# Five copies of the running counts in PSUM in an edge sort: one copy to SBUF for five chunks

## The chip, the cores and the metric

The kernel runs on one NeuronCore of one Trainium2 chip. The metric is the device time of one execution in microseconds; the kernel before has a median of 14442.03 us over 3 runs (14433.29 to 14450.2).

## The reference, cut to what matters

Four graph layers work on one graph of 12,500 nodes and 400,000 edges; each gathers node features by edge, makes a message, and adds the messages up by node.

```python
edge_index = jnp.stack([src, dst])
h = jnp.maximum(_layernorm(x, axis=-1), 0.0)
x = x + _L0_gnn_ref(h, edge_index, ...)          # x[s] * norm, segment_sum over d
...
x = x + _L1_gnn_ref(h, edge_attr_16, ..., src, dst, edge_type_90)
...
x = x + _L2_gnn_ref(h, edge_attr_4, edge_index, ...)
...
x = x + _L3_gnn_ref(h, src, dst, edge_weight)
```

Before the layers, the kernel sorts the edges by the pair of 128-node buckets that their destination and their source lie in: 98 x 98 pairs. This sort is what is changed. It is no part of the reference, and the order within a pair doesn't matter to it.

## The kernel before

A first pass (`hist`, to about 417 us) counts the edges of each pair of buckets; `cbase`, 98 x 98, holds the slot at which each pair begins. The sort itself walks over the edges in `NBE` = 125 blocks of 3200: `KE` = 25 chunks of 128 edges, one edge to a partition. `rec` in DRAM gets one record of 32 bytes per edge, at the slot of that edge. The slot is the running count of the edge's pair over all chunks before (`p_c`), plus the edge's rank among the equal keys of its own chunk.

For one block the steps are these, by the lines of the kernel before:

- ScalarE's queue issues the loads `keyb` (L508, 1.6 MB) and `db` (L511); SP's queue issues the loads of the edges' inputs (L503) and one piece of a clearing of DRAM buffers (L527, 1.5 MB).
- VectorE (DVE) makes `ohdt`, the one-hot of the destination bucket with buckets on partitions, in f32 (L516), the shifts and the packed word (L535 to L553), the product `pr` and its sum into `q` (L556, L557), and the one-hots `ohd` and `ohs` of destination and source bucket, in bf16 (L298, a helper that also makes `ohl`).
- 25 rounds, one for each chunk `k`: ScalarE copies the counts from PSUM, `c_sb <- p_c` (L573, 98 x 98 f32). PE adds the chunk's own counts to `p_c` (L574, `ohd` against `ohs`, bf16, accumulated in PSUM). PE looks up the counts for the chunk's edges, `p_l` (L576, `ohdt` against `c_sb`, f32). DVE makes the rank by comparing keys (`junk`, L579). The next copy has to wait until L574 has added, and L574 has to wait until the copy has read.
- After every five chunks DVE picks the count of each edge's source bucket: `own` (L583, 490 wide) and a reduction into `slot_f` (L584).
- After the 25 chunks DVE makes `ohl`, adds `slot_f` and `rank` (L589), and works out `slot` (L591 to L601). Then GpSimd (POOL) issues 25 indirect DMAs (L603), each of which scatters the 128 records of a chunk to `rec`.
- PE counts degrees of the block with 25 matmuls into `p_deg` (L475) from `ohd` and `ohl`, while the next block begins.

The tiles of the `sort` pool have two buffers each, those of `count` three, `p_l` three. `q` of a block shares its buffer with `q` of the block two earlier, and can be written when the scatters of that block have landed. A recording layer with a scheduler decides in which order the instructions of neighbouring blocks stand on each engine: for example DVE makes `ohdt` of the next block before it finishes `slot` of this one. On ScalarE the first copy of a block stands before that block's loads are issued, since it only needs the counts of the block before.

Of the kernel before, what the change touches and what calls it, by code (L numbers as in the profile page):

```python
# [30 lines left out]
F32 = mybir.dt.float32  # L31
# [4 lines left out]
ALU = mybir.AluOpType  # L36
AF = mybir.ActivationFunctionType
AX = mybir.AxisListType
# [6 lines left out]
P = 128  # L45
# [3 lines left out]
NB = 98  # L49
# [7 lines left out]
KE = 25  # L57
BE = P * KE
NBE = E // BE
UE = 5  # L60
KI = UE * KE

# [19 lines left out]
def gnn_kernel(  # L82
# [25 lines left out]
    nc = tc.nc  # L108
# [23 lines left out]
    ident = const.tile([P, P], F32, name="ident")  # L132
# [72 lines left out]
    def clear(acc, m, width):  # L205
        for c in range(0, width, 512):
            w = min(512, width - c)
            nc.tensor.matmul(acc[:m, c : c + w], zeros[:, :m], zeros[:, :w], start=True, stop=False,
                             skip_group_check=True)
# [59 lines left out]
    with ExitStack() as begin:  # L269
# [15 lines left out]
        cbase = base.tile([NB, NB], F32, name="cbase")  # L285
# [18 lines left out]
        with tc.tile_pool(name="hist", bufs=2) as hist, tc.tile_pool(name="hpsum", bufs=1, space=PSUM) as ps:  # L304
            p_cnt = ps.tile([NB, NB], F32, name="p_cnt")
            clear(p_cnt, NB, NB)
            for it in range(NBE // UE):
                e0 = it * UE * BE
                hi = {}
                for name, idx in (("d", dst), ("s", src)):  # L310
                    v = hist.tile([P, UE, KE], I32, name="v" + name)
                    nc.sync.dma_start(v, idx[e0 : e0 + UE * BE].rearrange("(u p k) -> p u k", u=UE, k=KE))
                    v = v.rearrange("p u k -> p (u k)")
# [9 lines left out]
                for v, row, dt in ((key, keyrow, F32), (hd, drow, BF16)):  # L323
# [4 lines left out]
                    nc.sync.dma_start(row[it * KI : (it + 1) * KI, :], tt)  # L328
                for u in range(UE):
                    sl = slice(u * KE, (u + 1) * KE)  # L330
                    ohd = hist.tile([P, KE, NB], BF16, name="ohd")
                    one_hot_n(ohd, hi["d"][:, sl, :], NB)
                    ohs = hist.tile([P, KE, NB], BF16, name="ohs")
                    one_hot_n(ohs, hi["s"][:, sl, :], NB)
                    for k in range(KE):
                        nc.tensor.matmul(p_cnt, ohd[:, k, :], ohs[:, k, :], start=False, stop=False,
                                         skip_group_check=True)
# [117 lines left out]
        with (  # L455
# [1 line left out]
            tc.tile_pool(name="count", bufs=3) as count,  # L457
            tc.tile_pool(name="spsum", bufs=1, space=PSUM) as ps,
        ):
            p_c = ps.tile([NB, NB], F32, name="p_c")  # L460
            nc.tensor.matmul(p_c, ident[:NB, :NB], cbase, start=True, stop=False, skip_group_check=True)
            p_deg = ps.tile([NB, P], F32, name="p_deg")
            clear(p_deg, NB, P)

# [8 lines left out]
            def count_degrees(oh):  # L473
                for k in range(KE if oh else 0):
                    mm = nc.tensor.matmul(p_deg, oh[0][:, k, :], oh[1][:, k, :], start=False, stop=False,  # L475
                                          skip_group_check=True)
                    if k == 0:
                        tc.keep_in_program_order(mm)
# [4 lines left out]
            for buf, src_z in ((buf1, zero_b), (buf2, zero_b), (buf3, zeros)):  # L483
                flat = buf.rearrange("(p g) c -> p (g c)", g=NG)
                m, step = flat.shape[1], src_z.shape[1]
                for c in range(0, m, 6 * step):
                    k, w = divmod(min(6 * step, m - c), step)
# [3 lines left out]
                    if w:  # L491
                        blank.append((flat[:, c + k * step : c + k * step + w], src_z[:, :w]))
            every = -(-len(blank) // (NBE - 1))

            degrees = None
            for blk in range(NBE):
                e0 = blk * BE
# [17 lines left out]
                ohdt = sort.tile([NB, BE], F32, name="ohdt")  # L515
# [47 lines left out]
                slot_f = sort.tile([P, KE], F32, name="slot_f")  # L563
                ohd = sort.tile([P, KE, NB], BF16, name="ohd")
                one_hot_n(ohd, hi["d"], NB, iota_p)
                ohs = sort.tile([P, KE, NB], BF16, name="ohs")
                one_hot_n(ohs, hi["s"], NB, iota_p)
                count_degrees(degrees)
                for kb in range(0, KE, 5):
                    p_l = ps.tile([P, 5, NB], F32, name="p_l", bufs=3)  # L570
                    for k in range(kb, kb + 5):
                        c_sb = count.tile([NB, NB], F32, name="c_sb")
                        nc.scalar.copy(c_sb, p_c)  # L573
                        nc.tensor.matmul(p_c, ohd[:, k, :], ohs[:, k, :], start=False, stop=False,  # L574
                                         skip_group_check=True)
                        nc.tensor.matmul(p_l[:, k - kb, :], ohdt[:, k * P : (k + 1) * P], c_sb,  # L576
                                         start=True, stop=True)
                        junk = count.tile([P, P], BF16, name="junk")
                        nc.vector.scalar_tensor_tensor(junk, keyb[:, k * P : (k + 1) * P], key[:, k : k + 1],  # L579
                                                       earlier_p, op0=ALU.is_equal, op1=ALU.mult,  # L580
                                                       accum_out=rank[:, k : k + 1])
                    own = count.tile([P, 5, NB], F32, name="own")
                    nc.vector.tensor_tensor(own, p_l, ohs[:, kb : kb + 5, :], op=ALU.mult)  # L583
                    nc.vector.tensor_reduce(slot_f[:, kb : kb + 5], own, axis=AX.X, op=ALU.add)  # L584
                ohl = sort.tile([P, KE, P], BF16, name="ohl")
                one_hot_n(ohl, lo_d, P, iota_p)
                degrees = (ohd, ohl)
# [24 lines left out]
        with (  # L612
# [51 lines left out]
            for g0 in range(0, NG, 35):  # L664
# [6 lines left out]
                for g in range(g0, g0 + nm):  # L671
                    nc.tensor.matmul(pm[:, g - g0, :], ht[:, (g - g0) * P : (g - g0 + 1) * P], mvx[:, g, :],
                                     start=True, stop=True)
# [625 lines left out]
```

## Time and profile before

| what | before |
| --- | --- |
| median of 3 runs | 14442.03 us |
| profiled execution, its own time | 14454.86 us |
| its span, first to last instruction | 14452.8 us |
| mean granted PE clock | 0.599 of full |
| PE, DVE, ACT, POOL busy | 50%, 64%, 17%, 49% |
| first and last start of L603 (the sort's scatters) | 479.1 us, 6969.2 us |
| L573 copies, one | 3125, 241 ns |
| L574 matmuls, one | 3125, 254 ns |
| L576 matmul passes (f32 takes two), one | 6250, 457 ns |
| L603 indirect DMAs on POOL, one | 3125, 966 ns |

The profile is of one execution. A group's row gives its busy time, the mean of one instruction in ns, and the idle time of its engine just before its instructions, with what ended most of that. "PEld" is PE's loading of weights, which overlaps its matmuls; ends of matmuls are modelled. "issue" and "remote" are waits for which the profile shows no instruction that ended them. In timeline rows the columns are the start in us, the duration in us, engine, line, operation and tiles, and in brackets the idle time before it with what ended it.

### The profile page before, as it was taken

How to read it: one execution, taken by the hardware profiler on the slowest of the kernel's cores; microseconds unless marked ns; L12 is line 12 of the kernel's file. 1: busy time of each engine (PE TensorE's matmuls, PEld its weight loads, DVE VectorE, ACT ScalarE, POOL GpSimd, SP SyncE). 2: the span in 40 equal slices, each digit the busy share in tenths (PEclk: the TensorE clock that was granted, in tenths of full speed). 3: DMA queues.
4: the chain of work that ended last, by engine and by line, in shares of the span. 5: the costliest groups of instructions: out<-in, count | busy, mean ns of one | idle time of the engine just before them, and what ended most of it. 6: DMA issues, size and time to landing. Idle time of an engine off the chain costs nothing. (4 is left out here: it accounts for less than half of the span.)

```text
span 14452.8 us, 284351 instructions
## 1 busy us (share of the span) xinstructions
PE 7195.8 (50%) x112895; PEld 6405.0 (44%) x112895; DVE 9312.5 (64%) x18267; ACT 2509.1 (17%) x7316; POOL 7108.7 (49%) x8252
## 2 busy tenths in 40 slices
PE   5433333333333333333223622688888566656677
PEld 5333333333333333333122422577776555546666
DVE  8544444444444444444445634999999989995799
ACT  0111111111111111111122222000000542201344
POOL 0344444444444444444386287377777425520476
PEclk7555555555555555555555555599999559955555
DMA  3222222222222222221576387433333326646543
GB/s 86 91 83 83 83 83 76 78 80 80 83 83 83 83 83 83 83 83 63 170 238 207 115 273 245 137 96 95 95 95 91 114 85 203 192 125 200 162 123 110
DMA packets 1100964, 1704.92 MB, mean 118 GB/s; under 512 B 660792, under 2 KB 727909, under 8 KB 1080779
## 3 DMA queue, kind: packets, MB, share of 16 engines
q1 hardware_dynamic: 746151, 737.61, 17.2%
q10 hardware_dynamic: 164704, 715.37, 14.6%
q0 software_dynamic: 188704, 233.01, 5.2%
q8 instruction: 906, 14.84, 0.4%
q14 instruction: 499, 4.09, 0.1%
HBM read 1079.99 MB, written 555.86 MB: 113 GB/s over the span
## 5 line engine op out<-in xcount | busy, mean ns | idle before, releaser
L603 POOL DMA_INDIRECT rec<-q,slot x3125 | 3019.6, 966 | 3532.6 <-issue 3469.1
L576 PEld LDWEIGHTS p_l<-c_sb,ohdt 98*128 98x128 f32 x6250 | 1606.3, 318 | 3288.2 <-issue 3039.2
L583 DVE TENSOR_TENSOR own<-p_l,ohs 128x490 f32<-128x490 f32 x625 | 418.1, 669 | 3390.4 <-PE p_l L576 2183.9
L574 PE MATMUL p_c<-ohs,ohd 128*98 128x98 bf16 x3125 | 794.2, 254 | 3518.0 <-issue 1512.5
L576 PE MATMUL p_l<-c_sb,ohdt 98*128 98x98 f32 x6250 | 1999.9, 457 | 242.5 <-DVE gran L591 200.0
L715 POOL DMA_INDIRECT buf<-msg,place x1188 | 1544.4, 1300 | 819.5 <-DVE msg L249 341.4
L573 ACT COPY c_sb<-p_c 98x98 f32<-98x98 f32 x3125 | 753.7, 241 | 5671.1 <-remote 2414.7
L769 DVE TENSOR_TENSOR oh<-lo,row 128x2304 bf16<-128x2304 bf16 x1070 | 1413.0, 1346 | 77.5 <-PEq L739 31.7
L1007 PE MATMUL pw<-wt,ot 128*128 128x256 bf16 x10692 | 1267.3, 273 | 374.5 <-DVE pr L1011 333.4
L1007 PEld LDWEIGHTS <-ot 128*128 128x128 fp8e4 x10692 | 1043.2, 98 | 575.6 <-issue 457.7
L1011 DVE TENSOR_TENSOR pr<-pw,hg 128x1536 f32<-128x1536 f32 x594 | 1041.3, 1753 | 145.6 <-POOL mm L1026 137.9
L747 PE MATMUL pg<-xg,o 128*128 128x16 bf16 (+1 forms) x33156 | 980.0, 173 | 288.6 <-DVE o L700 159.9
L747 PEld LDWEIGHTS <-o 128*128 128x128 fp8e4 x33156 | 938.6, 101 | 322.3 <-DVE o L700 169.5
L574 PEld LDWEIGHTS <-ohd 128*98 128x98 bf16 x3125 | 626.7, 201 | 693.7 <-DVE ohd L298 426.6
L579 DVE SCALAR_TENSOR_TENSOR junk<-keyb,key,fixed 128x128 bf16<-128x128 f32 x3125 | 918.3, 342 | 0.0
L919 PE MATMUL pg<-xg,o 128*128 128x48 bf16 x7128 | 328.4, 215 | 1095.3 <-DVE o L700 456.8
L786 PEld LDWEIGHTS <-oh 128*128 128x128 bf16 x22464 | 661.3, 104 | 433.9 <-DVE oh L769 270.2
L715 POOL DMA_INDIRECT buf<-mm,place x396 | 740.3, 1870 | 121.2 <-issue 67.3
L919 PEld LDWEIGHTS <-o 128*128 128x128 fp8e4 x7128 | 297.9, 118 | 1125.8 <-DVE o L700 486.0
L1023 DVE TENSOR_TENSOR pr<-pr 128x2304 f32<-128x2304 f32 (+1 forms) x396 | 772.8, 1951 | 0.1
L800 PE MATMUL pa<-m,oh 128*128 128x48 bf16 x11772 | 588.5, 215 | 355.4 <-DVE oh L769 320.8
L1216 POOL DMA_INDIRECT xj<-buf,place x396 | 393.6, 994 | 644.7 <-ACT lo L756 543.2
(362 smaller groups left out, 12943.8 us busy)
## 6 DMA issues: line engine op xcount, KB each, us to landing
o<-oh_s ACTq DMA_DIRECT2D x396, 576.0 KB
keyb<-keyrow ACTq DMA_DIRECT2D x125, 1600.0 KB
buf<-zeros SPq DMA_DIRECT2D x120, 1536.0 KB
m<-buf SPq DMA_DIRECT2D x218, 432.0 KB
db<-drow ACTq DMA_DIRECT2D x125, 612.5 KB
mf<-buf SPq DMA_DIRECT2D x109, 576.0 KB
er<-erow SPq DMA_DIRECT2D x109, 576.0 KB
t<-srow SPq DMA_DIRECT2D x99, 576.0 KB
```

The costliest lines, as they stand in the source:

```text
L573: nc.scalar.copy(c_sb, p_c)
L574: nc.tensor.matmul(p_c, ohd[:, k, :], ohs[:, k, :], start=False, stop=False, skip_group_check=True)
L576: nc.tensor.matmul(p_l[:, k - kb, :], ohdt[:, k * P : (k + 1) * P], c_sb, start=True, stop=True)
L579: nc.vector.scalar_tensor_tensor(junk, keyb[:, k * P : (k + 1) * P], key[:, k : k + 1], earlier_p, op0=ALU.is_equal, op1=ALU.mult, accum_o ...
L603: st = nc.gpsimd.indirect_dma_start(out=rec_rows, out_offset=bass.IndirectOffsetOnAxis(ap=slot[:, k : k + 1], axis=0), in_=q[:, k, :], in_ ...
L715: st = nc.gpsimd.indirect_dma_start(out=buf, out_offset=bass.IndirectOffsetOnAxis(ap=place[:, g : g + 1], axis=0), in_=msg, in_offset=None)
L747: nc.tensor.matmul(pg[:, k, :], o[:, k * P : (k + 1) * P], xg[:, (g + k // G) % LD, c, :], start=c == 0, stop=c == 2)
L769: nc.vector.tensor_tensor(oh.rearrange("p k (m t) -> p k m t", t=2), lo2[:, v : v + S, None, :].to_broadcast([P, S, P // 2, 2]), row[:, No ...
L786: nc.tensor.matmul(pa[:, v + i], oh[:, i * G + k, :], msg[:, i * G + k][:, c], start=k + c == 0, stop=k + c == G + 1)
L1007: nc.tensor.matmul(pw[:, k].rearrange("p i o -> p (i o)"), st["ot"][:, (k0 + k) * P : (k0 + k + 1) * P], wt3[:, c, :], start=c == 0, stop= ...
L1011: nc.vector.tensor_tensor(pr[:, sl], pw, hg[:, sl, :F, None].to_broadcast([P, S // 3, F, F]), op=ALU.mult)
L1023: e.tensor_add(pr[:, :, :n], pr[:, :, :n], pr[:, :, n : 2 * n])
```

## The change

`p_c` gets five copies side by side in PSUM (`KB` = 5, 490 columns), all begun with `cbase`. Copy number i of a group of five chunks is to hold the counts up to chunk i of the group. So before the copy to SBUF, chunk j is added to the copies after j only (`add_counts(..., j + 1, KB)`); then one ScalarE copy takes all five, 490 columns; then chunk j is added to the copies up to j (`add_counts(..., 0, j + 1)`), so that all five are equal again for the next group. The chunk's one-hot `ohs` is the moving operand, repeated over the copies by a broadcast. A group now has nine matmuls into `p_c` with 10 + 15 = 25 copies' worth of columns, where it had five matmuls of one copy each. The five `p_l` matmuls follow, each with its own part of `c_sb`. Ranks, `own` and the reduction are as before. The change also moves instructions, since the scheduler places them anew: no `c_sb` copy stands in the block before any more, and DVE's and ScalarE's work for neighbouring blocks is interleaved otherwise.

```diff
+KB = 5
...
-            p_c = ps.tile([NB, NB], F32, name="p_c")
-            nc.tensor.matmul(p_c, ident[:NB, :NB], cbase, start=True, stop=False, skip_group_check=True)
+            p_c = ps.tile([NB, KB, NB], F32, name="p_c")
+            nc.tensor.matmul(p_c, ident[:NB, :NB], cbase[:, None, :].to_broadcast([NB, KB, NB]),
+                             start=True, stop=False, skip_group_check=True)
+
+            def add_counts(ohd, ohs, k, a, b):
+                if a < b:
+                    nc.tensor.matmul(p_c[:, a:b, :], ohd[:, k, :],
+                                     ohs[:, k, None, :].to_broadcast([P, b - a, NB]), start=False, stop=False,
+                                     skip_group_check=True)
...
-                for kb in range(0, KE, 5):
-                    p_l = ps.tile([P, 5, NB], F32, name="p_l", bufs=3)
-                    for k in range(kb, kb + 5):
-                        c_sb = count.tile([NB, NB], F32, name="c_sb")
-                        nc.scalar.copy(c_sb, p_c)
-                        nc.tensor.matmul(p_c, ohd[:, k, :], ohs[:, k, :], start=False, stop=False,
-                                         skip_group_check=True)
-                        nc.tensor.matmul(p_l[:, k - kb, :], ohdt[:, k * P : (k + 1) * P], c_sb,
+                for kb in range(0, KE, KB):
+
+                    for j in range(KB):
+                        add_counts(ohd, ohs, kb + j, j + 1, KB)
+                    c_sb = count.tile([NB, KB, NB], F32, name="c_sb")
+                    nc.scalar.copy(c_sb, p_c)
+                    for j in range(KB):
+                        add_counts(ohd, ohs, kb + j, 0, j + 1)
+                    p_l = ps.tile([P, KB, NB], F32, name="p_l", bufs=3)
+                    for k in range(kb, kb + KB):
+                        nc.tensor.matmul(p_l[:, k - kb, :], ohdt[:, k * P : (k + 1) * P], c_sb[:, k - kb, :],
                                          start=True, stop=True)
                         junk = count.tile([P, P], BF16, name="junk")
...
```

More of the change, by code (lines that the diff above doesn't have):

```diff
@@ L581, in gnn_kernel @@
                                                        accum_out=rank[:, k : k + 1])
-                    own = count.tile([P, 5, NB], F32, name="own")
-                    nc.vector.tensor_tensor(own, p_l, ohs[:, kb : kb + 5, :], op=ALU.mult)
-                    nc.vector.tensor_reduce(slot_f[:, kb : kb + 5], own, axis=AX.X, op=ALU.add)
+                    own = count.tile([P, KB, NB], F32, name="own")
+                    nc.vector.tensor_tensor(own, p_l, ohs[:, kb : kb + KB, :], op=ALU.mult)
+                    nc.vector.tensor_reduce(slot_f[:, kb : kb + KB], own, axis=AX.X, op=ALU.add)
                 ohl = sort.tile([P, KE, P], BF16, name="ohl")
```

## The prediction

> **What bounds the kernel now.** I read the page first, then the timeline of one block of the sort, then windows within that block. The sort's 125 blocks run from 435 to about 6970 us: the slot of a block (L601) is first written at 478.0 us and last at 6937.8 us, so a block takes (6937.8 - 478.0) / 124 = 52.1 us. The page's groups:
>
> ```profile
> L603 POOL DMA_INDIRECT rec<-q,slot x3125 | 3019.6, 966 | 3532.6 <-issue 3469.1
> L574 PE MATMUL p_c<-ohs,ohd 128*98 128x98 bf16 x3125 | 794.2, 254 | 3518.0 <-issue 1512.5
> L573 ACT COPY c_sb<-p_c 98x98 f32<-98x98 f32 x3125 | 753.7, 241 | 5671.1 <-remote 2414.7
> ```
>
> No engine is full here: POOL, PE and ScalarE each wait longer than they work. The timeline shows why. One round is copy (0.24 us), matmul into p_c, next copy:
>
> ```profile
> 3006.34 0.24 ACT L573 COPY c_sb<-p_c 98x98 f32<-98x98 f32 x1 [2.60 <-remote]
> 3006.64 0.24 PE L574 MATMUL p_c<-ohs,ohd 128*98 128x98 bf16 x1 [2.09 <-ACT c_sb L573]
> 3008.51 0.24 ACT L573 COPY c_sb<-p_c 98x98 f32<-98x98 f32 x1 [1.92 <-PE p_l L576]
> ...
> 3016.32 0.24 ACT L573 COPY c_sb<-p_c 98x98 f32<-98x98 f32 x1 [2.59 <-remote]
> 3021.94 0.24 ACT L573 COPY c_sb<-p_c 98x98 f32<-98x98 f32 x1 [5.38 <-remote]
> ...
> 3035.31 0.24 ACT L573 COPY c_sb<-p_c 98x98 f32<-98x98 f32 x1 [0.35 <-PE p_c L574]
> 3035.91 0.24 ACT L573 COPY c_sb<-p_c 98x98 f32<-98x98 f32 x1 [0.35 <-PE p_c L574]
> ```
>
> At 3035 a round takes 0.60 us. At 3006 to 3030 it takes 2 to 8 us: the matmul ends at 3006.88, but the copy that waits for it starts at 3008.51. From copy to matmul it stays 0.05 us; only PE's message to others is late. The windows say when (columns: PE, PEld, DVE, ACT, POOL busy, PE clock, DMA share, GB/s):
>
> ```profile
> 3001.00:3002.00 1.00, 1.00 (x7) 1.00 (x7) 1.00 (x8) 0.37 (x2) 0.69 (x2) 0.50 1.04 371
> 3008.00:3010.00 2.00, 0.76 (x3) 0.59 (x3) 0.00 (x0) 0.24 (x1) 1.69 (x2) 0.50 0.04 4
> 3034.00:3036.00 2.00, 2.00 (x13) 2.00 (x11) 1.61 (x10) 0.82 (x4) 0.00 (x0) 0.50 0.00 0
> ```
>
> Rounds are slow while POOL's scattered writes (L603) are alone on the DMA engines, and quick when POOL is silent or bulk transfers run beside it. Why, the trace does not say; I use the size. From the first p_c matmul (2999.98) to the last own (3038.79) the loop takes 38.8 us; 25 quick rounds would take 25 x 0.6 = 15. The 24 us more lie on about 11 slow rounds: 2.2 us for each late message. Call it e; single rounds show 0.9 to 7.
>
> After the loop comes a tail on DVE:
>
> ```profile
> 3038.79 0.67 DVE L583 TENSOR_TENSOR own<-p_l,ohs 128x490 f32<-128x490 f32 x1 [0.39 <-PE p_l L576]
> 3042.48 3.54 DVE L516 SCALAR_TENSOR_TENSOR ohdt<-db,part,fixed 98x3200 f32<-98x3200 bf16 x1
> 3048.70 0.96 POOL L603 DMA_INDIRECT rec<-q,slot  x1 [20.86 <-issue]
> 3050.84 1.43 DVE L298 TENSOR_TENSOR ohs<-his,iota_p 128x2450 bf16<-128x2450 bf16 x1
> 3052.32 0.24 PE L574 MATMUL p_c<-ohs,ohd 128*98 128x98 bf16 x1 [5.43 <-DVE ohs L298]
> ```
>
> So a block is 38.8 us of loop and 13.5 us of tail (3038.79 to 3052.32). POOL's burst of 25 (31.5 us) has 21 us of slack.
>
> **The change, part by part.** Call A the matmuls before a group's copy (4+3+2+1 = 10 copies wide), B those after it (15 wide), L the five p_l matmuls.
>
> PE's price, and the copy's. Three rows, the PE ones at the same half clock:
>
> ```profile
> 3041.24 2.83 PE L475 MATMUL p_deg<-ohl,ohd 128*98 128x128 bf16 x25 [2.49 <-DVE ohl L298]
> 11839.71 2.02 PE L1059 MATMUL pe<-we_sb,ht 16*128 16x96 f32 x8
> 11838.87 0.43 ACT L1061 COPY te<-pe 128x320 f32<-128x320 f32 x1 [1.03 <-PE pe L1059]
> ```
>
> 25 matmuls of 128 columns, each with its weights, take 2.83 us, of which 0.31 is the length of the last (mean of this group): 2.52 / 24 = 0.105 us each, 0.82 ns a column. A is 980 columns, 0.81 us; B is 1470, 1.21 us. A moving operand that is repeated by a broadcast is in no row; I price its columns like these, between half (the page's slices at clock 0.9) and double, that is from 1 us less to 2 us more a group. An f32 matmul is two passes; eight passes of 96 columns take 2.02 us with a drain of 0.42, so 0.23 a pass, and L's ten take 2.3 us. What p_l's 98 columns and 98 rows of weights cost back to back no row shows: from a little under this to the 0.29 us between the two passes of a p_l matmul now, which would add 0.6 us a group. I take 0.23, the row with passes back to back.
>
> The copy grows from 98 to 490 columns. The row above takes 0.43 us for 320; against 0.24 for 98 that is 0.84 ns a column, so 0.57 us, once instead of five times 0.24.
>
> A group without lateness: A 0.81, drain, message and copy 0.84 (0.18 of drain, the L574 row's 0.25 less its 0.08 of columns; 0.04 for a prompt message; 0.57; 0.05 back), B 1.21, L 2.3: 5.2 us, against 5 x 0.6 = 3.0 now. So without late messages the change would lose 2.2 x 5 = 11 us a block. It gains by waiting for one message a group, not five. The built program has PE signal twice a group, after A and after L: 10 signals a block instead of 50.
>
> Late messages. The first A finds bulk transfers or POOL barely begun, so it costs nothing; four groups pay e. The fourth group's L ends at 4 x 5.2 + 3e = 20.8 + 3e = 27.4 us after the first matmul.
>
> Moved work. The order of DVE's instructions changes more than the diff says. ohl, spare_t, spare, ohdt, the first shifts of the next block and pr (about 7.6 of the tail's 13.5 us) now stand before the last own, beside PE's last group; what is left after it, up to ohs, is 13.5 - 7.6 = 5.9 us. Between the fourth and the last own stand, by their spacing in the timeline: own 0.6, spare_t 0.7, a reduce 0.6, spare 0.6, ohdt 3.5, seven small ones 0.6, pr 0.5, in all 7.1 us. So the last own starts at the later of 27.4 + e + 7.1 = 36.7 (DVE) and 27.4 + 5.2 + 2e = 37.0 (PE). Plus 5.9: a block of 42.9 us. One A falls beside keyb's transfer (now issued on ScalarE's queue between the fourth and fifth copy), and bulk beside it made the rounds quick, so I take off half an e: 42 us.
>
> The other queues. The slot is now written after ohs of the next block, so POOL's burst starts about 1.3 us after the first matmul instead of 3.6 before it. q of the next block (DVE's reduce, ScalarE's two copies) waits for that burst: 1.3 + 31.5 (2996.37 to 3027.85 in the timeline) + about 0.9 until the last write lands (DMA activity ends before 3030), then 3.8 us of reduce, small steps, ohd and ohs: 37.5 us. This is the floor of a block, below 42, so POOL's wait is hidden; if the loop gets shorter, it is next. SP's loads and keyb fill buffers for the block after next and keep most of a block as slack. The degree matmuls (2.8 us) hide under the 5.9 us.
>
> A rule to weigh: the clock stays at 0.50 at 3034 to 3036 with PE busy for all of the 2 us, and had done so for over ten; so I price A, B and L at half clock. (The Trainium skill, "TensorE: Matmul & The Clock Gate", Part 1, says that a window of some 3.4 us of sustained work lifts the clock to full; B, L and the next A are 4.3 us in a row, and by that rule a group would shrink towards 3 us and the block to POOL's floor, about 12630 in all.)
>
> Sum: (52.1 - 42) x 124 = 1250 us. The profiled execution took 14454.9 us (span 14452.8), 12.8 above the median; 14454.9 - 1250 - 12.8 = 13192, so 13190. The order after the sort is unchanged.
>
> **The rivals.** *POOL's floor decides* (messages of 0.9 us, as in the shortest slow round): 37.5 us a block, 14.6 x 124 = 1810 us less, 12630. For it: fewer signals, keyb's transfer. Against: the mean is 2.2, and POOL's burst now covers the whole loop.
>
> *The messages get later* and the change loses: a block is 31.9 + 5e, so 52.1 is reached at e = 4.0. Rounds late in POOL's burst already show 5.6 and 7.7 us (3016.32, 3021.94, 3029.64). If all hops pay 5.6, a block is 59.9 us: 970 us more, 15410. Against: only two or three of a block's rounds are like that; the mean is 2.2.
>
> *In between*: e = 3.2, half the hops late in the burst: 47.9 us, 520 us less, 13920.
>
> **How the numbers follow.** About forecast (40 to 45 us a block): 0.45. POOL's floor or near it: 0.28. Long messages but still faster: 0.15. No change to within 0.2% (what can be told from no change): 0.03. Slower: 0.09. Faster is 0.45 + 0.28 + 0.15 = 0.88. The range runs from POOL's floor, 12630, to e = 3.2, 13920; beyond lie the two slower cases and the end of the third.
>
> **What would show it.** 625 copies of 490 columns near 0.57 us; p_c matmuls of 2450 columns a group; PE busier by about 2 us a group; between A and its copy about 2 us while POOL writes, 0.04 otherwise; ohdt before the last own; POOL's idle time down from 21 to about 10 us a block. Wrong if the gap from A to the copy is above 4 us, if PE's group takes over 6 us without it, or if POOL has no idle time left.

## The result and the profile after

The change makes the kernel slower: 14671.7 us (median of 4 runs, 14661.7 to 14684.1) against 14444.2 of before (4 runs), a ratio of 1.0159 [1.0141, 1.0176]. The profiled execution of after has a span of 14668.5 us and a mean clock of 0.621. A block of the sort takes 53.8 us in place of 52.1, so (53.81 - 52.10) x 125 = 214 of the 228 us lie in the sort.

One thing must be known ahead of the experiments. The runs met the chip in two conditions. In one (before and after above, e5 to e7, e12 to e14, e18) before takes 14438 to 14477 us; in the other (e1 to e4, e8 to e11, e15 to e17) the same program takes 11859 to 11863. I call them the late and the prompt condition. Every comparison below is with runs of before in the same set.

The page of after; the columns are busy time, mean of one instruction in ns, and idle time ahead of them with what ended most of it:

```profile
L615 POOL DMA_INDIRECT rec<-q,slot x3125 | 3030.9, 970 | 3734.7 <-issue 3331.4
L467 PE MATMUL p_c<-ohs,ohd 128*98 128x392 bf16 (+4 forms) x5625 | 1429.0, 410 | 3834.9 <-ACT c_sb L583 2299.9
L583 ACT COPY c_sb<-p_c 98x490 f32<-98x490 f32 x625 | 355.2, 568 | 6264.9 <-remote 3532.4
```

The copies are a fifth as many and each is as long as forecast, but ScalarE's idle time ahead of them has grown from 5671 to 6265 us, and GpSimd's ahead of the scatters from 3533 to 3735. The timeline of one block:

```profile
3007.89 0.97 PE L467 MATMUL p_c<-ohs,ohd 128*98 128x392 bf16 x4 [8.40 <-DVE ohs L299]
3008.95 0.57 ACT L583 COPY c_sb<-p_c 98x490 f32<-98x490 f32 x1 [12.49 <-PE p_c L467]
...
3012.84 1.02 PE L467 MATMUL p_c<-ohs,ohd 128*98 128x392 bf16 x4
3013.95 0.57 ACT L583 COPY c_sb<-p_c 98x490 f32<-98x490 f32 x1 [4.43 <-PE p_l L588]
...
3017.84 1.02 PE L467 MATMUL p_c<-ohs,ohd 128*98 128x392 bf16 x4
3021.34 0.57 ACT L583 COPY c_sb<-p_c 98x490 f32<-98x490 f32 x1 [6.82 <-issue]
...
3025.22 0.94 PE L467 MATMUL p_c<-ohs,ohd 128*98 128x392 bf16 x4
...
3039.61 0.97 POOL L615 DMA_INDIRECT rec<-q,slot  x1 [0.30 <-issue]
3043.82 0.67 DVE L595 TENSOR_TENSOR own<-p_l,ohs 128x490 f32<-128x490 f32 x1 [22.39 <-remote]
3044.61 0.57 ACT L583 COPY c_sb<-p_c 98x490 f32<-98x490 f32 x1 [22.70 <-remote]
...
3048.49 1.02 PE L467 MATMUL p_c<-ohs,ohd 128*98 128x392 bf16 x4
3049.60 0.57 ACT L583 COPY c_sb<-p_c 98x490 f32<-98x490 f32 x1 [4.43 <-PE p_c L467]
```

Number the A's of a block 0 to 4. A0 and A1 reach the copy at once. A2 ends at 3018.86 and its copy starts at 3021.34: 2.5 us late. A3 ends about 3026.2 and its copy starts at 3044.61, 18.4 us later; the own that waits for the L ahead of it (own of group 2) is held as well. The last scatter is issued at 3039.61 (to 3040.58), so both signals arrive 3 to 4 us after GpSimd's burst is over. The trace's own record of TensorE's semaphore has updates at 3043.80 and 3044.53, and the copy starts 0.08 us after the second: it is the update that is late, not ScalarE in seeing it. (Ends of matmuls are modelled, so the trace cannot tell a late message from a matmul whose results are late.) A4 is prompt again. While A3's signal is held nothing runs except the scatters (columns: us, PE, PEld, DVE, ACT, POOL busy, PE clock, DMA share, GB/s):

```profile
3012.00:3014.00 2.00, 1.86 (x9) 1.62 (x9) 0.92 (x4) 0.05 (x1) 1.51 (x2) 0.50 0.02 2
3034.00:3036.00 2.00, 0.00 (x0) 0.00 (x0) 0.00 (x0) 0.00 (x0) 1.39 (x3) 0.50 0.02 2
```

In 93 of the 124 blocks after the first it is A3's signal that is held for more than 10 us, in 14 it is A2's, in 14 A4's, in 3 none. Over the blocks after the first the five hops from A to its copy have means of 0.09, 0.54, 5.45, 12.98 and 2.26 us, 21.3 us a block.

### The profile page after: what moved, and what is told of

The parts are those of the page before. It is cut to its first block, busy times and chain, and to the rows that moved or that the text cites. A ratio compares the mean times of both kernels' runs of the same rounds, so it can differ in the third digit from the quotient of the medians.

```text
span 14668.5 us, 287194 instructions
## 1 busy us (share of the span) xinstructions
PE 7590.2 (52%) x115395; PEld 6756.8 (46%) x115395; DVE 9317.2 (64%) x18267; ACT 2101.3 (14%) x4816; POOL 7125.9 (49%) x8252
## 5 line engine op out<-in xcount | busy, mean ns | idle before, releaser
L467 PE MATMUL p_c<-ohs,ohd 128*98 128x392 bf16 (+4 forms) x5625 | 1429.0, 410 | 3834.9 <-ACT c_sb L583 2299.9
L467 PEld LDWEIGHTS <-ohd 128*98 128x98 bf16 x5625 | 919.8, 189 | 4004.8 <-issue 3327.3
L588 PEld LDWEIGHTS p_l<-c_sb,ohdt 98*128 98x128 f32 x6250 | 1415.5, 319 | 114.7 <-DVE ohdt L525 3.0
L588 PE MATMUL p_l<-c_sb,ohdt 98*128 98x98 f32 x6250 | 1365.8, 401 | 2.3 <-DVE ohdt L525 2.3
L583 ACT COPY c_sb<-p_c 98x490 f32<-98x490 f32 x625 | 355.2, 568 | 6264.9 <-remote 3532.4
L798 PEld LDWEIGHTS <-oh 128*128 128x128 bf16 x22464 | 661.5, 104 | 433.6 <-DVE oh L781 272.3
L812 PEld LDWEIGHTS <-oh 128*128 128x128 bf16 x11772 | 503.1, 117 | 445.8 <-DVE oh L781 433.2
```

What stands on the lines that cost most here:

```text
L467: nc.tensor.matmul(p_c[:, a:b, :], ohd[:, k, :], ohs[:, k, None, :].to_broadcast([P, b - a, NB]), start=False, stop=False, skip_group_chec ...
L798: nc.tensor.matmul(pa[:, v + i], oh[:, i * G + k, :], msg[:, i * G + k][:, c], start=k + c == 0, stop=k + c == G + 1)
L812: nc.tensor.matmul(pa[:, v + i].rearrange("p c f -> p (c f)"), oh[:, i * G + k, :], msg[:, i * G + k].rearrange("p c f -> p (c f)"), start ...
```

## The experiments

Three questions: whether the loss is late signals or the longer work of TensorE; what sets the lateness; and whether a kernel is to be had that is faster than both. "Age" is the time since the first scatter of GpSimd's run.

### e1 to e4: the counts of a signal, and a loop behind the burst

The built program lets TensorE signal once after A, adding 4 to its semaphore, and once after L, adding 10; before adds 1 each time. Were such an addition delivered count by count, A3 would be held for that (theory C; theory A says that the age alone decides). e1 and e2 change the counts and nothing else, by renumbering the built program (the signals of the sort and every wait on them):

```diff
     with tile.TileContext(nc) as tc:
         gnn_kernel(tc, *args)
+    recount(nc, lambda i, n, ins: 1)        # e1, on after: each signal adds 1
+    recount(nc, lambda i, n, ins: 7 * n)    # e2, on before: each adds 7 times as much
```

e3 (on after, shown here) and e4 (the same on before) let the loop begin when the last scatter is out:

```diff
                 count_degrees(degrees)
+                if burst_over is not None:
+                    tc.keep_in_program_order(
+                        nc.tensor.matmul(p_c[:, 0, :], burst_over, ohs[:, 0, :], start=False, stop=False,
+                                     skip_group_check=True))
                 for kb in range(0, KE, KB):
...
                     tc.add_to_no_dep_group("rec", st.ins)
+                burst_over = sort.tile([P, NB], BF16, name="burst_over")
+                tc.keep_in_program_order(nc.gpsimd.memset(burst_over, 0.0))
```

> The kernel after, with one thing changed: the signals that TensorE sends in the sort count 1 each, where the matmul that closes A adds 4 and the one that closes L adds 10 (every wait's value is renumbered to match; no instruction is added, removed or moved). Theory C (counts): a signal that adds n is delivered as n single counts one after the other, and while the scatters have the DMA engines to themselves one count takes about 0.4 us at an age of the burst of 6 to 9 us, 1 us up to 18 us and 2 to 3.5 us after that (before's hops, two counts a round). So A2 would be about 2 us late, A3 2.5, A4 6, nothing would be held to the end of the burst, a block would take 41 to 44 us in place of 53.8, and the kernel 13000 to 13500 us. Theory A (age): a signal that is sent 14 us or more into the burst is held until the burst is over, whatever it adds: A3 stays 16 us late and the time 14670, within 40.

> The kernel before, with every signal of TensorE in the sort adding 7 where it added 1 (waits renumbered to match; nothing else). Theory C (counts): a round puts 14 counts in place of 2 on their way, so that after the four quick rounds beside the bulk transfers only one to three rounds get through before the burst ends, and some 19 rounds of 0.6 us are left behind it in place of 12: 4 to 7 us more a block, 14900 to 15400 us. Theory A (age): no change, 14440 within 40.

> The kernel after, with the loop made to begin when the previous block's scatters are out (a matmul of zeros ahead of A0 waits for a 128x98 memset that GpSimd does behind its 25th scatter), so that no signal of the loop is sent during the burst. Both theories: all five hops prompt, groups of 5.0 us, loop 25 us from A0 to the last own. A block is the burst 31.9 + about 3 for what is still on its way + 25 + 4 from the last own to the first scatter: 63 to 65 us, 15800 to 16100 us in all. Theory W (plain work): the 1.8 us a block that the change loses are TensorE's longer groups and not the signals; then this kernel would also lie only about 230 us above the same edit of before.

> The kernel before with the same edit (the loop begins when the previous block's scatters are out). All 25 rounds quick at 0.594 us, loop 15 us; a block is 31.9 + about 3 + 15 + 4: 53 to 55 us, 14550 to 14800 us. So without late signals the new loop is 10 us a block slower than the old one, 1250 us in all, where the change as made loses 228: it must have got back some 1000 us in late signals. Theory W says the two kernels with this edit differ by about 230 us.

Measured: before 11858.6 us in this set. e1 12644.5, ratio 1.0664 [1.0646, 1.0681]; e2 11869.9, 1.0007 [0.9997, 1.0018]; e3 15741.2; e4 15076.3 (one run each).

This was the prompt condition, so e1 and e2 could not speak on lateness: there is none. In e2's trace the mean hop from p_c to the copy is 0.04 to 0.06 us in every bin of age up to 21 us, where before in the late condition has up to 7 us. Its rounds, and GpSimd's row:

```profile
2396.39 0.24 ACT L573 COPY c_sb<-p_c 98x98 f32<-98x98 f32 x1 [0.39 <-PE p_c L574]
2397.02 0.24 ACT L573 COPY c_sb<-p_c 98x98 f32<-98x98 f32 x1 [0.39 <-PE p_c L574]
```

```profile
L603 POOL DMA_INDIRECT rec<-q,slot x3125 | 3022.5, 967 | 1020.1 <-issue 923.4
```

A scatter takes 967 ns here and 966 in the late condition, a copy 242 and 241: the work is as long, the signals differ. A block of e2 is 31.8 us, 31.5 of burst and a gap of 0.3: without lateness the old loop is bound by GpSimd alone. (52.1 - 31.8) x 125, about 2540 us, is nearly all of the 2586 between the two conditions of before (14444.2 and 11858.6).

e3 and e4 give the plain price of the two loops: blocks of 63.1 and 57.7 us, 665 us in all, with e4's loop at 14.2 us and e3's at 14 to 20 from its first to its last copy. The new loop is slower by 5.3 us a block, half of the 10 expected, because many of its groups ran at a full clock in 3.0 us and not in 5.0 (178 of the 496 distances between the copies of a block are under 3.3 us). Theory W, which wanted 230 us, is out by its own number. What e1 loses to before in the prompt condition is looked at in e17.

### e5 to e7: after once more, and a third buffer for q

```diff
-                q = sort.tile([P, KE, R], F32, name="q")
+                q = sort.tile([P, KE, R], F32, name="q", bufs=3)
```

> The kernel after itself, beside before on the same chip, since e2 found before at 11860 us where it had been 14440, with no signal of TensorE late. Where before takes 11860: theory D (VectorE's order) says that before's block there is GpSimd's burst and nothing else (31.6 us + a gap of 0.3), and that after cannot follow, because the slots of a block stand in VectorE's queue behind the q reduce of the next one, which waits until the burst is over and its q buffer free: a gap of 6.3 us, 125 x 6.1 = 765 us more, 12620 to 12660. Where before takes 14440: 14670 again, within 40.

> The kernel after with three buffers for q in place of two, nothing else; the order of VectorE's instructions stays the same. Where before takes 11860: theory D says that the q reduce then waits for nothing, GpSimd's gap falls from 6.3 us to about 0.3, a block is 31.9 us and the kernel as fast as before within 60 us. Theory P (TensorE's longer groups, 25 us of loop in place of 15) says that the buffer changes nothing: 12640. Where before takes 14440: the held signal ends the block, not the q reduce, so 14600 to 14700 by both.

> The kernel of e6 once more for one look at another time. Where before takes 11860: as e6 within 30 us. Where before takes 14440: as e6 within 40 us.

Measured: before 14477.2; e5 14680.3, ratio 1.0142 [1.0125, 1.0159]; e6 14687.1, 1.0146 [1.0129, 1.0163]; e7, e6's kernel again in spite of its name, 14688.9. The late condition: the result above is repeated, and the buffer changes nothing, as expected if the held signal ends the block and not the wait for q (hops of e6: 0.10, 0.58, 5.62, 12.79, 2.24).

### e8 and e9, then e12: the counts again

> The kernel of e1 (after, every signal of TensorE in the sort counting 1 where it counted 4 or 10) once more, for a time when before takes 14440 and signals are late. Theory C (counts): a signal that adds n is delivered as n counts one after the other, about 1 us each in the middle of the burst; A3 then is 2 to 3 us late in place of 16, a block 41 to 44 us, 13000 to 13500 in all. Theory A (age): a signal's lateness depends on how long GpSimd's run of scatters has lasted when it is sent, whatever it adds: 14670 within 40, A3 16 us late. Where before takes 11860 it tells nothing new: 12640.

> The kernel of e2 (before, every signal of TensorE in the sort adding 7 for 1) once more, for a time when before takes 14440. Theory C: 14 counts a round in place of 2, one to three rounds in the burst behind the first four, 14900 to 15400. Theory A: as before within 40. Where before takes 11860 it tells nothing new: 11870.

Both met the prompt condition (before 11859.6): 12636.2 and 11864.3 (one run each), as e1 and e2. Without lateness an addition of 7 costs what an addition of 1 costs. e12 met the late condition:

> The kernel of e1 and e8 (after, every signal of TensorE in the sort counting 1), once more for a time when before takes 14440. Theory C (counts): A3 2 to 3 us late in place of 16, a block 41 to 44 us, 13000 to 13500. Theory A (age): 14670 within 40. Where before takes 11860: 12640.

Measured: 14672.0 us (one run), before 14459.6. The copies of one block of e12, each signal counting 1:

```profile
3006.72 0.57 ACT L583 COPY c_sb<-p_c 98x490 f32<-98x490 f32 x1 [12.37 <-PE p_c L467]
3011.72 0.57 ACT L583 COPY c_sb<-p_c 98x490 f32<-98x490 f32 x1 [4.43 <-PE p_l L588]
3021.16 0.57 ACT L583 COPY c_sb<-p_c 98x490 f32<-98x490 f32 x1 [8.88 <-remote]
3042.35 0.57 ACT L583 COPY c_sb<-p_c 98x490 f32<-98x490 f32 x1 [20.61 <-remote]
3047.16 0.57 ACT L583 COPY c_sb<-p_c 98x490 f32<-98x490 f32 x1 [4.25 <-DVE own L595]
```

The same picture: prompt, prompt, some us, held, prompt. Hops of 0.09, 0.55, 5.70, 12.82, 2.20. So the counts are not what holds after's signals, and theory C, which I had thought the best explanation, is out.

### e10, e11 and e13, e14: the burst cut into five runs

e10 and e13 are after, with e6's third buffer for q as well; e11 and e14 are before.

```diff
+            still = sort.tile([P, 3136], F32, name="still", bufs=1)
...
                     tc.add_to_no_dep_group("rec", st.ins)
+                    tc.keep_in_program_order(st)
+                    if k % 5 == 4 and k < KE - 1:
+                        tc.keep_in_program_order(nc.gpsimd.memset(still, 0.0))
```

> The kernel after with three buffers for q, and with GpSimd's burst cut into five runs of five scatters (6.3 us each) by a memset of 128x3136 f32 behind each of the first four (an estimate of 2.8 us from 1.41 us for 128x1568). Where before takes 14440: if lateness goes by the age of the unbroken run (theory A), every run starts anew, the five hops are each less than 1 us late, the loop ends within the burst of 31.6 + 4 x 2.8 = 43 us and a block is 43 to 46 us: 13300 to 13700. If it goes by the number of scatters since the block's first, pauses or not, A3 is held to the end of a burst that is 11 us longer: a block of 62 to 66, 15700 to 16200. Where before takes 11860: the pauses only lengthen the burst, 43 us a block, 13250 to 13400.

> The kernel before with the same pauses. Where before takes 14440: by theory A all 25 rounds run at 0.6 to 0.9 us beside runs of five, the loop is done inside the burst, and a block is the burst, 43 to 46 us: 13300 to 13700. By the count of scatters: rounds of 2 to 7 us through a burst of 43 us, a block of 56 to 64 us, 14900 to 16000. Where before takes 11860: 43 us a block, 13250 to 13400.

These met the prompt condition: 13171.1 and 13151.6 us (before 11859.6), 42.2 us a block in both. A pause takes 2.73 us, and all that they do there is to lengthen the burst.

> The kernel of e10 (after, three buffers for q, the burst in five runs of five scatters with memsets between) for a time when before takes 14440. If lateness goes by the age of the unbroken run: hops below 1 us, a block of 43 to 46 us, 13170 (as without lateness) to 13700. If by the scatters since the block's first: A3 held to the end of a burst 11 us longer, 15700 to 16200. Where before takes 11860: 13170.

> The kernel of e11 (before with the same pauses) for a time when before takes 14440. By the age of the unbroken run: rounds of 0.6 to 0.9 us, 13150 to 13700. By the scatters since the block's first: 14900 to 16000. Where before takes 11860: 13150.

Measured in the late condition: e13 13258.4 us, ratio to before 0.9169 [0.9142, 0.9195]; e14 13245.9, 0.9160 [0.9134, 0.9187]. A block is 42.2 us in both, exactly what it is in the prompt condition: the lateness has stopped costing anything in the sort. (The 87 and 94 us that e13 and e14 take more than e10 and e11 lie behind it.) One loop of e13:

```profile
2938.91 0.57 ACT L584 COPY c_sb<-p_c 98x490 f32<-98x490 f32 x1 [4.20 <-PE p_l L589]
2938.97 2.74 POOL L623 MEMSET still<- 128x3136 f32 x1
...
2941.93 0.57 ACT L584 COPY c_sb<-p_c 98x490 f32<-98x490 f32 x1 [2.46 <-PE p_c L467]
...
2944.95 0.57 ACT L584 COPY c_sb<-p_c 98x490 f32<-98x490 f32 x1 [2.45 <-PE p_c L467]
...
2947.30 0.59 PE L467 MATMUL p_c<-ohs,ohd 128*98 128x392 bf16 x4
2947.92 2.74 POOL L623 MEMSET still<- 128x3136 f32 x1
...
2949.18 0.57 ACT L584 COPY c_sb<-p_c 98x490 f32<-98x490 f32 x1 [3.66 <-PE p_c L467]
```

Three copies follow their A's at once. The last A (2947.30 to 2947.89) falls at the end of the second run, and its copy comes 1.3 us late, inside the next pause. In e14 the same shows in the small: rounds at 0.59 us to the end of a run, and then the one late one, let through 1.2 us into the pause:

```profile
2938.32 0.24 ACT L574 COPY c_sb<-p_c 98x98 f32<-98x98 f32 x1 [0.35 <-issue]
2938.92 0.24 ACT L574 COPY c_sb<-p_c 98x98 f32<-98x98 f32 x1 [0.35 <-issue]
2940.27 2.73 POOL L611 MEMSET still<- 128x3136 f32 x1
2941.43 0.24 ACT L574 COPY c_sb<-p_c 98x98 f32<-98x98 f32 x1 [2.27 <-PE p_l L577]
```

And no bulk transfer is needed for that. Two windows of e13's loop, the second with a DMA share of 0.01:

```profile
2935.00:2938.00 3.00, 3.00 (x15) 2.77 (x14) 0.00 (x0) 0.00 (x0) 2.10 (x3) 0.50 0.15 30
2941.20:2944.20 3.00, 2.29 (x21) 2.09 (x21) 2.31 (x10) 0.57 (x1) 2.45 (x3) 1.00 0.01 1
```

So the lateness needs a long run of scatters without a pause (theory A), in either kernel; GpSimd being busy is not enough, since signals come through while it is at its memset. Whether the time without a pause counts, or scatters that pile up and drain in the pause, these runs do not tell: a pause also makes scatters rarer. The two kernels are 8% faster than before in the late condition, but 11% slower in the prompt one; and with the pauses the five copies in PSUM bring nothing, since both kernels then are GpSimd's burst.

### e15, e16 and e18: shorter pauses

The tile of the memset has 784 columns in place of 3136; it takes 0.77 us. e16, on after, again has the third buffer for q.

> The kernel before with the four pauses of e11 cut from 2.73 us to an estimated 0.7 (a memset of 128x784 f32). Where before takes 14440: if the end of a run is enough (theory A with a quick recovery), the loop stays inside the burst of 31.6 + 4 x 0.76 = 34.6 us, a block is 34.9 to 36, 12300 to 12550. If a backlog has to drain that is as long as the 3 to 4 us that signals still come late after an unbroken burst, the runs act as one: 14440 + 4 x 0.76 x 125 = 14800. Between the two I expect the first. Where before takes 11860: 34.9 us a block, 12230 to 12300.

> The kernel after with three buffers for q and the same short pauses. Where before takes 14440: if the end of a run is enough, 34.9 to 37 us a block, 12300 to 12700; if not, one hop held to the burst's end as in after, 14670 to 15100. Where before takes 11860: 12240 to 12320.

> The kernel of e15 (before, four pauses of an estimated 0.7 us in the burst) for a time when before takes 14440. If the end of a run is enough, the loop stays inside the burst of 34.0 us (e15) and a block is 34.3 to 36: 12200 to 12500. If a backlog has to drain first, as the 3 to 4 us suggest in which signals still come late after an unbroken burst, the five runs act as one: rounds of 2 to 7 us, 14600 to 14800. The pauses of 2.73 us (e14) left hops of 2 us at most, so I expect 12200 to 12500, with some blocks longer. Where before takes 11860: 12180 as e15.

Measured, prompt condition (before 11863.0): e15 12177.4, ratio 1.0265 [1.0248, 1.0282], blocks of 34.3 us; e16 12349.2, 1.0416 [1.0398, 1.0433], 35.7 us. Late condition (before 14438.3): e18 13530.3, 0.9370 [0.9354, 0.9386]. The scatters' rows of e14 and e18:

```profile
L604 POOL DMA_INDIRECT rec<-q,slot x3125 | 3024.9, 968 | 944.5 <-issue 881.9
```

```profile
L604 POOL DMA_INDIRECT rec<-q,slot x3125 | 3035.1, 971 | 2194.2 <-issue 2130.5
```

e18's block is 44.5 us in place of 34.3: hops from an age of 9 us on are 0.5 to 1.3 us in the mean, against 2 to 7 in before and at most 0.3 with the long pauses. 0.77 us lets out a part of what 2.73 us lets out whole. The runs between pauses are of five scatters in both, so the length of a run alone does not set the lateness; the length of the pause counts too. My expectation (12200 to 12500) was too good, the other (14600 to 14800) too bad. It is a compromise between the two conditions (2.7% lost or 6.3% won), and no kernel that I ran beats before in both.

### e17: the third q buffer where no signal is late

> The kernel of e6 (after with three buffers for q) once more. Where before takes 11860: theory D (the slots stand behind the q reduce) says 31.9 us a block and the time of before within 60 us; theory P (TensorE's longer groups) says 12640 as e1. Where before takes 14440 it tells nothing new: 14690.

Measured: 12148.7 us (one run), before 11863.0. What VectorE's q reduce (L566) waits for in e1, then in e17 (total us, times):

```profile
L566 DVE TENSOR_REDUCE q<-pr x125: 540/572/573, 456.0 to 5161.9; 128x25 f32<-128x400 f32 x125
...
  DMA rec<-q,slot: 643.3, 99
```

```profile
L566 DVE TENSOR_REDUCE q<-pr x125: 557/571/572, 455.4 to 4670.3; 128x25 f32<-128x400 f32 x125
...
  DMA rec<-q,slot: 1.2, 7
```

The third buffer takes the wait away, GpSimd's gap between bursts falls from 6.6 to 2.6 us and a block from 38.1 to 34.1: (38.1 - 34.1) x 125 = 500 of the 786 us by which e1 lies above before. The other 286 stay. The window of one block reads: five copies 5.0 us apart, the last p_l matmul's end, then 8 us of VectorE's steps to the next A0, about 35 us where groups take 5.0 us, above the burst's 31.8. Over all blocks it is so: where the five copies span about 20 us (58 blocks), the next block's first copy comes 35.3 us after this one's and GpSimd's gap is 4.2 us; where they span about 14 us, at a full clock (29 blocks), these are 31.8 and 0.8. So both theories hold a part: D about two thirds, P (TensorE's longer groups) the rest.

The two conditions together answer the first question. The late condition costs before 2586 us, after 14671.7 - 12644.5 = 2027 (e1 for its prompt time, since e12 shows that the counts do nothing), and after with the third buffer 14687.1 - 12148.7 = 2538. So with a fifth as many signals lateness costs 560 us less, or, with the third buffer, about as much as in before: there are fewer late signals, and each is later. The 228 us that the change loses are the 786 us that it is slower without lateness, less those 560. These are differences between whole kernels, not parts that a run took out one by one: the wait for q, 500 of the 786, costs nothing in the late condition (e6).

## Why the prediction was wrong, step by step

**The failing term: "2.2 us for each late message. Call it e".** The sum itself nearly held: it gave a block of 31.9 + 5e for long messages, for four copies and the last own. The four copies waited 0.54 + 5.45 + 12.98 + 2.26 = 21.2 us in the mean, and 31.9 + 21.2 is 53.1, where 53.8 was measured; ahead of the last own VectorE had no idle time in 108 of 124 blocks, so that wait was for its own work. That is 5.3 us for each of the four in place of 2.2, and 4.25 over the sum's five terms, just above the break-even of 4.0 that the rival *The messages get later* named. The sign that the text gave for its being wrong, more than 4 us from A to the copy, came at A2 and A3. The text chose the mean over before's slow rounds, and lateness is no constant. Mean hop in us by the age of the burst when the signal was sent, from the two profiles (p_c to copy, A to copy), and e2's:

| age, us | 3-6 | 6-9 | 9-12 | 12-15 | 15-18 | 18-21 | 21-24 | 24-27 |
| --- | --- | --- | --- | --- | --- | --- | --- | --- |
| before, late condition | 0.05 | 0.86 | 2.1 | 1.9 | 2.5 | 3.4 | 6.1 | 7.1 |
| after, late condition | 0.18 | 5.3 | 4.0 | 11.9 (8) | 18.5 | 16.4 | none sent | 9.7 (2) |
| e2 (before), prompt condition | 0.06 | 0.04 | 0.04 | 0.04 | 0.04 | 0.04 | 0.04 (1) | none sent |

It grows along the burst, in before from 0.05 to 7.1 us (numbers in brackets: few signals in that bin). Before's mean is drawn down by many early rounds; after's hops sit at ages of about 0, 5, 10 and 17 to 19. This much stood in the trace of before, had the rounds been set against the start of the burst. That after's are later than before's even at equal age did not. e12 excludes the counts as the reason, e13 shows that the unbroken run of scatters is needed for it; why a signal that is sent at 18 us is delivered after 3 us in before and only behind the burst in after stays open (before sends two signals a round and after two in 5 us; I did not test whether later signals push earlier ones through).

**The cause I read off the windows** ("slow while POOL's scattered writes are alone on the DMA engines, and quick when ... bulk transfers run beside it") was a coincidence of place: in before bulk transfers run at ages of 0 to 6 us, when signals are prompt anyway. After's A1, sent at 3013.86, reaches its copy in 0.09 us with a DMA share of 0.02 (the window 3012 to 3014 above), and e13 has prompt hops at 0.01. From this wrong cause came "One A falls beside keyb's transfer ... so I take off half an e": keyb is issued on ScalarE's queue behind the held copy (3045.89), after the burst, and helps nobody.

**Right steps, and two signs that failed.** A group without lateness: 5.2 forecast, 5.0 measured (median distance of the first two copies). The copy: 0.57, measured 568 ns. L's ten passes: 2.3, measured 2.29. A and B from first to last: 0.97 to 1.02 and 1.39, with their drain. The tail from the last own to the next A0: 5.9, measured 3055.78 to 3061.78 = 6.0. The burst starts 1.1 us after A0 begins (1.3 forecast). But GpSimd's idle time was to fall from 21 to 10 us a block and is 22, by the held signal, and TensorE was to be busier by 2 us a group and is by (7590.2 - 7195.8) / 625 = 0.6.

**The floor.** The rival *POOL's floor decides* gave 37.5 us a block and 12630 us. In the prompt condition that is what came out: e1 38.1 and 12644.5. But there before takes 11860, for its slots are ready before the burst ends. The move of the slot behind the next block's q and ohs, which I priced as hidden, is not hidden there: of the 6.3 us that a block is longer, the third buffer for q takes back 4.0 (e17).

**The clock.** The text priced all groups at half clock and set a rule against it: the Trainium skill, "TensorE: Matmul & The Clock Gate", Part 1, has a window of about 3.4 us of sustained work lift the clock. The row of 3034 to 3036 was a weaker sign than the text made of it: the clock had been at 0.50 for over ten us, but TensorE worked without a break only from about 3032 (0.68 us busy from 3030 to 3032). In e1 about half of the third and fourth groups run at full clock, 3.0 us apart (61 and 63 of 124); of the first, 109 stay at 0.50 and 5.0 us. The windows of e13 above show both within 10 us (0.50, then 1.00). A group at half clock leaves TensorE a gap of 0.71 us in every 5.0, ahead of its B. In e1's trace the clock changes in steps of 3.41 us, and 103 of its 123 rises in the sort come at the end of a step without any gap, though 19 other such steps (ends of matmuls are modelled) brought none. So the rule fits where a whole step falls between two gaps, and that is a matter of place; in after, held, it was of no use.

## What to carry to other kernels

A wait's price is not a mean to be multiplied: set each slow wait against the time since the thing that is beside it began, and price the new waits where they will stand. Fewer round trips help only if the ones left do not move to a worse place, and an engine that another order makes wait (here the slots behind the next block's q) can cost more than the trips. Where signals are late beside a long run of one engine's DMA issues, breaking the run is a cheap thing to try, and the time of the unchanged kernel has to be taken in the same set.

## What the runs showed of the hardware

- TensorE's signals can be late by up to 20 us while GpSimd issues 25 indirect scatters in a row (31.5 us), although ScalarE's take 0.05 us at any age (327 in before at ages over 9 us). VectorE's take 0.05 us too, but only ones sent in the first 5 us of an unbroken run are seen. The same program meets the chip with this lateness (14440 us) or without any (11860); a scatter takes 966 and 967 ns, a copy 241 and 242. What decides it no trace shows.
- Pauses of 2.73 us after every fifth scatter end the cost of it in the sort; with pauses of 0.77 us a block takes 44.5 us (52.1 without pauses, 34.3 for the burst with them).
- An addition of 4, 7 or 10 to a semaphore costs no more than one of 1 (7: e2 and e9 against before, without lateness; 4 and 10: after against e12, with it).
- A moving operand repeated by a broadcast costs TensorE what its columns cost: B's 1470 columns take 1.39 us with their drain at half clock, about as forecast from plain rows.
